# Mamba stages with compute engines kept in source order, lags of a slot or more between maker and reader, and one pair's X in SBUF

## The chip, the cores and the metric

The kernel runs on one core of a Trainium2 chip. The metric is the device time of one execution in microseconds (us). The core has five engines with a queue each: TensorE (PE, matmul), VectorE (DVE), ScalarE (ACT), GpSimd (POOL), and SyncE (SP), which here issues nearly all DMAs. An engine runs its queue in order; what it needs from another engine it waits for on a semaphore.

## The reference

Four layers over an image x of 4 x 96 x 64 x 64: a Mamba block with fusion and batch norm (layer 0), an SSD block (layer 1), a second Mamba block like the first (layer 2), a ConvNeXt block (layer 3). The change touches layers 0 and 2. With L = 4096 positions, DIN = 192, 16 states:

```python
def _mamba_block(seq, ...):
    h = (seq - mu) * rsqrt(var + EPS) * ln_g + ln_b
    xs, z = split(h @ in_w, 2)
    xc = silu(sum(conv_w[:, k] * xp[:, k:k + L, :] for k in range(4)) + conv_b)
    dbl = xc @ xproj_w                                  # dt (6), Bm (16), Cm (16)
    delta = softplus(dt @ dt_w + dt_b)
    dA = exp(delta[..., None] * A)
    dBx = delta[..., None] * Bm[:, :, None, :] * xc[..., None]
    hstates = associative_scan(dA, dBx)                 # h[t] = dA[t] * h[t-1] + dBx[t]
    y = (einsum('blds,bls->bld', hstates, Cm) + Dp * xc) * silu(z)
    return y @ out_w

for i in range(2):
    seq = seq + _mamba_block(seq, ...)
gp = relu(x.mean((2, 3)) @ gp_w.T + gp_b)               # one vector per image
out = fus_w @ concat([seq, gp]) + fus_b                 # then batch norm over all images
```

## The kernel before, in words

**Steps, groups, slots.** `mamba_fusion` (L467) keeps X, all four images as 96 channels x 4096, in SBUF. Images are handled in pairs. A step is one chunk of T = 512 positions of one pair in one of the two sub-layers: 2 pairs x 2 sub-layers x 8 chunks = 32 steps for each Mamba stage, 64 in the program. Two images of 192 channels fill three tiles of 128 partitions (j = 0, 1, 2). A step has 24 groups (`units`, L385), eight for each j; a group is two scans of 128 partitions (8 channels x 16 states) by 512. `Scan.run` (L383) writes the order of the work out by hand: it goes through slots n, one for each group, and in slot n calls the stages of different groups with fixed lags.

**The stages of a group g before** (lag in slots after its scan): `load` (-4) issues on SP the DMAs that broadcast 8 rows of delta (dd, written to DRAM by the front) over 16 states into da; a "DMA group" (6 of 24) also loads du from dg. `decay` (-2): ScalarE, two exps in place in da. `spread` (-1): for ordinary groups two matmuls (L313) that spread du into the PSUM tile bs; for DMA groups ScalarE's exps into bs and GpSimd's product du x B (L308). `scan` (0): for ordinary groups VectorE's product bs x B (L335), then two VectorE scans (L340) into hs, GpSimd's product hc = hs x C (L342), and ScalarE's copy of the last column into carry (L345). `sums` (+2): TensorE adds hc over states into py (L361); once per j a matmul adds D x xc (L355). `close` (+3): VectorE multiplies py by silu(z) (L369). `project` (+4): two matmuls into po (L377), VectorE adds po to X (L381). `fuse` (+5, second sub-layer only): matmul pf (L510), ScalarE adds the bias (L511), VectorE takes bn_stats (L512), SP stores.

**The front** (`mamba_front`, L155) makes the next step's tiles while this one scans. It is a generator; `PACE` (L256) says how many of its pieces each slot takes, and `LEAD` (L257) that it starts four slots before the step ends. Its pieces: layer norm (matmuls pc and pv, ScalarE's Square and rsqrt, VectorE's product L184, GpSimd's affine L185); twelve conv taps as matmuls (L194) with ScalarE copies into xz and a Silu; z (L204); the projection dbl (L217, L222), written to DRAM and read back broadcast as bc (L226, L245); and for each j softplus (L260): TensorE's pt, ScalarE's Abs, Exp, Ln, VectorE's max and add (L267), ScalarE's Identity back into the PSUM tile (L268), VectorE's second instruction (L270) on that PSUM tile and u, GpSimd's addition (L271) and product du (L248), and the stores dd and dg (L251).

**What sets the order.** The code is written against a framework that puts in semaphores and allocates buffers by name (`bufs` = how many; a new tile waits until the old one's users are done). It also sorts: each engine's queue is the result of a scheduler that may put a later instruction ahead of an earlier one that isn't ready by its own estimate. The lags and `PACE` are thus a wish; nothing before the change holds an engine to them.

## Time and profile before

| | |
|---|---|
| three runs | 9810.94, 9849.05, 9851.49 us (median 9849.05) |
| profiled execution | 9796.82 us, span 9795.1 us, mean granted TensorE clock 0.941 |
| busy, share of the span | PE 86%, DVE 83%, POOL 70%, ACT 56% |
| first Mamba stage | first scan at 78.1 us, batch norm's result at 3060 us |
| SSD stage | to about 6160 us |
| second Mamba stage | first scan at 6246 us, batch norm's result at 9210 us |
| ConvNeXt stage | to the end |
| DMA | 71% busy and 204 GB/s between 300 and 2700 us |

How to read the profile: a row of groups names line, engine, operation, output <- inputs, shapes and count; then busy us and mean ns of one; then the engine's idle time just before these instructions and what ended most of it. The slice rows cut the span into 40 equal parts; a digit is the busy share in tenths (9 is 90% or more). A row of a stretch (A:B) gives its length, then the busy us and number of instructions of PE, PE's weight loads, DVE, ACT and POOL, the granted clock, the DMA share and GB/s. A matmul of this kernel in fp32 is two records. A timeline row begins with start and length in us.

### The profile page before, as it was taken

How to read it: one execution, taken by the hardware profiler on the slowest of the kernel's cores; microseconds unless marked ns; L12 is line 12 of the kernel's file. 1: busy time of each engine (PE TensorE's matmuls, PEld its weight loads, DVE VectorE, ACT ScalarE, POOL GpSimd, SP SyncE). 2: the span in 40 equal slices, each digit the busy share in tenths (PEclk: the TensorE clock that was granted, in tenths of full speed). 3: DMA queues.
4: the chain of work that ended last, by engine and by line, in shares of the span. 5: the costliest groups of instructions: out<-in, count | busy, mean ns of one | idle time of the engine just before them, and what ended most of it. 6: DMA issues, size and time to landing. Idle time of an engine off the chain costs nothing. (4 is left out here: it accounts for less than half of the span.)

```text
span 9795.1 us, 110014 instructions
## 1 busy us (share of the span) xinstructions
PE 8426.9 (86%) x32750; PEld 3475.8 (35%) x32750; DVE 8142.4 (83%) x11036; ACT 5527.9 (56%) x10516; POOL 6879.1 (70%) x4573
## 2 busy tenths in 40 slices
PE   7888889888887988998888889788888888888678
PEld 1222212222212776776766767212212222222122
DVE  7999999999995666666666667699999999999887
ACT  5666666665663555555555555466666665666345
POOL 6888888888884555555555555588888888888511
PEclk8999999999997999999999999799999999999789
DMA  6677776777774222222222222576777776776653
GB/s 184 201 205 201 205 207 201 203 202 205 206 208 130 73 67 82 83 66 83 82 73 73 86 68 60 157 204 201 207 206 205 211 203 198 210 205 201 166 119 84
DMA packets 808930, 1525.65 MB, mean 156 GB/s; under 512 B 126190, under 2 KB 131722, under 8 KB 804491
## 3 DMA queue, kind: packets, MB, share of 16 engines
q1 hardware_dynamic: 805258, 1513.50, 54.4%
q8 instruction: 260, 4.26, 0.2%
q10 hardware_dynamic: 3072, 5.11, 0.1%
q14 instruction: 340, 2.78, 0.1%
HBM read 1222.99 MB, written 148.50 MB: 140 GB/s over the span
## 5 line engine op out<-in xcount | busy, mean ns | idle before, releaser
L342 POOL TENSOR_TENSOR hc<-hs,bc 128x1024 f32<-128x1024 f32 x1536 | 3610.9, 2358 | 625.5 <-DVE hs L340 545.8
L340 DVE TENSOR_TENSOR_SCAN hs<-da,carry,bs 128x512 f32<-128x512 f32 x2016 | 2466.5, 1264 | 81.0 <-DVE bs L335 2.8
L107 ACT ACTIVATE da<-da,w_a 128x512 f32<-128x512 f32 x2304 | 1616.9, 716 | 1251.7 <-DMA da<-dd 1191.7
L361 PE MATMUL py<-hc,selsum 128*32 128x512 f32 x6144 | 1797.8, 639 | 445.9 <-POOL hc L342 438.9
L313 PE MATMUL bs<-du,seldu 64*128 64x512 f32 x4608 | 1565.3, 675 | 216.0 <-DVE hs L340 203.7
L335 DVE TENSOR_TENSOR bs<-bs,bc 128x1024 f32<-128x1024 f32 x1152 | 1397.7, 1213 | 166.6 <-PE bs L313 163.1
L308 POOL TENSOR_TENSOR du<-du,bc 128x1024 f32<-128x1024 f32 x384 | 905.3, 2358 | 260.3 <-DMA du<-dg 141.0
L361 PEld LDWEIGHTS py<-hc,selsum 128*32 128x32 f32 x6144 | 239.8, 110 | 1791.8 <-POOL hc L342 1097.0
L917 DVE TENSOR_SCALAR seg<-dr,dac 128x128 f32<-128x128 f32 x1536 | 641.2, 451 | 281.9 <-PE y L962 279.5
L313 PEld LDWEIGHTS bs<-du,seldu 64*128 64x128 f32 x4608 | 444.0, 195 | 1205.2 <-DVE hs L340 864.4
L933 POOL TENSOR_TENSOR seg<-seg,cb 128x384 f32<-128x384 f32 x512 | 515.7, 1009 | 475.5 <-DVE cb L932 409.3
L194 PE MATMUL pu<-h,w_conv 96*128 96x512 f32 (+3 forms) x2048 | 833.4, 627 | 8.5 <-ACT rs L107 8.4
L340 DVE TENSOR_TENSOR_SCAN hs<-bs,carry,du 128x512 f32<-128x512 f32 x672 | 823.6, 1260 | 6.2 <-issue 3.2
L868 PE MATMUL front<-pk,sconv 128*128 128x512 f32 x1536 | 755.2, 609 | 27.7 <-ACT z L856 23.8
L972 POOL TENSOR_TENSOR y<-y,xs 128x192 f32<-128x192 f32 x496 | 295.3, 595 | 603.8 <-DVE y L971 587.9
L985 ACT ACTIVATE y<-yz 128x192 f32<-128x192 f32 x512 | 186.1, 363 | 906.2 <-DVE yz L984 905.5
L937 POOL TENSOR_TENSOR xs<-pre,coef 128x576 f32<-128x576 f32 x512 | 598.9, 1175 | 54.0 <-ACT pre L112 24.8
L879 PE MATMUL front<-sconv,pk 128*128 128x192 f32 x3072 | 572.0, 330 | 55.8 <-DVE pre L884 50.5
L345 ACT COPY carry<-hs 128x2 f32<-128x2 f32 x1344 | 250.9, 187 | 566.1 <-DVE hs L340 562.3
L879 PEld LDWEIGHTS front<-sconv,pk 128*128 128x128 f32 x3072 | 496.7, 190 | 87.7 <-DVE pre L884 76.8
L107 ACT ACTIVATE bs<-da,w_a 128x512 f32<-128x512 f32 x768 | 522.0, 680 | 3.1 <-DVE hs L340 1.6
L962 PEld LDWEIGHTS y<-xs,seg 128*128 128x128 f32 x3072 | 437.7, 204 | 142.0 <-issue 80.7
(209 smaller groups left out, 13623.5 us busy)
## 6 DMA issues: line engine op xcount, KB each, us to landing
da<-dd SPq DMA_DIRECT2D x3072, 256.0 KB
du<-dg SPq DMA_DIRECT2D x768, 256.0 KB
dr<-rows SPq DMA_DIRECT2D x256, 384.0 KB
bc<-rows SPq DMA_DIRECT2D x256, 256.0 KB
dd<-delta SPq DMA_DIRECT2D x192, 256.0 KB
dg<-du SPq DMA_DIRECT2D x192, 256.0 KB
pk<-xn SPq DMA_DIRECT2D x128, 384.0 KB
pk<-xn SPq DMA_DIRECT2D x128, 256.0 KB
```

Source lines behind the costliest of these rows:

```text
L107: self.last = self.scalar.activation(out, in_, func, **kw)
L194: nc.tensor.matmul(pu[r0:r1], lhsT=wt["conv"][:kk, tap, d0:d1], rhs=h[:kk, b, ds(tap, T)], start=(tap == 0), stop=(tap == 3),)
L308: nc.gpsimd.tensor_tensor(g["du"], g["du"], self.b_or_c(g, 0), ALU.mult)
L313: nc.tensor.matmul(g["bs"][:, i], lhsT=self.sel["du"][rows, g["half"], g["q"]], rhs=g["made"]["du"][rows, g["j"]], start=True, stop=True,)
L335: nc.vector.tensor_tensor(dbx, dbx, self.b_or_c(g, 0), ALU.mult)
L340: nc.vector.tensor_tensor_scan(hs[:, i], da[:, i], dbx[:, i], init, ALU.mult, ALU.add)
L342: nc.gpsimd.tensor_tensor(g["hc"], hs, self.b_or_c(g, 1), ALU.mult)
L361: nc.tensor.matmul(py[rows], lhsT=self.sel["sum"][:, g["q"]], rhs=g["hc"][:, i], start=(g["q"] == 0), stop=(g["q"] == NQU - 1),)
L868: nc.tensor.matmul(p, lhsT=self.conv[:, i, DI + q * DST : DI + (q + 1) * DST], rhs=pk[:, i, ds(c * T, T)], start=(i == 0), stop=(i == 2),)
L879: nc.tensor.matmul(p, lhsT=pk[:, i, ds(c * Q, Q)], rhs=self.conv[:, i, :DI], start=(i == 0), stop=(i == 2),)
L917: nc.vector.tensor_scalar(seg[:, h], g["pair"]["dr"][:, c % 2 * NH + h], made["dac"][:, n0 + h : n0 + h + 1], 0.0, ALU.subtract, ALU.min,)
L937: nc.gpsimd.tensor_tensor(xs, x.to_broadcast([P, 3, NH, HD]), coef.to_broadcast([P, 3, NH, HD]), ALU.mult)
```

## The change

Seven parts, all in the Mamba stages.

1. In `run`, after each slot, every instruction of the four compute engines is tied behind the one traced before it on its engine (`IN_ORDER`, an edge without a semaphore). SP isn't included.
2. Lags: load -5, hc and the carry copy become a stage of their own (`after`, +1), product du x B at -2, sums +3, close +4, project +4, `keep` +5, `spread_out` +6. Buffers: da 6 to 8, hs and hc 3 to 4, ua and lg 2. `LEAD` 5, other `PACE`.
3. The front's layer norm and softplus are skewed so that each piece reads what an earlier piece made. pv moves to the PSUM tile of po.
4. Softplus's Identity goes to an SBUF tile w instead of back into PSUM; VectorE's second instruction reads w and u.
5. The add into X is done by TensorE (identity x X into po first); ScalarE copies po to X. In the second sub-layer the fuse weight is multiplied into the out weight once, and fus x X takes the identity's place, so there is no fuse matmul.
6. bn_stats goes: sums come from ScalarE's accumulator outputs, squares from an added Square.
7. X holds one pair; pair 1's slices are loaded as pair 0's are finished, and the other pair's means come from pieces loaded through da tiles.

```diff
@@ mamba_front
-        sq = work.tile([P, T], F32, tag="ua", name="sq")[:C]
...
+    for n in range(4):
+        if n >= 2:
+            dst = h[:C, n - 2, 3 : 3 + T]
+            nc.vector.tensor_tensor(dst, centered[n - 2][0], roots[n - 2], ALU.mult)
...
+        if 1 <= n < 3:
+            pv = psum.tile([P, T], F32, tag="po", name="pv", bufs=1)[:C]
...
+        if n < 2:
+            pc = bank("pc")[:C]
...
     nc.scalar.activation(dbl, pd, AF.Identity, bias=wt["one"])
+    yield
...
+    for n in range(5):
+        if n >= 2:
+            j = n - 2
+            delta, lost = kept.pop(0)[:2]
+            nc.gpsimd.tensor_tensor(delta, delta, lost, ALU.add)
+            nc.gpsimd.tensor_tensor(du[:, j], delta, xz[:, j], ALU.mult)
...
+        if 1 <= n < 4:
+            softplus_rest(nc, *kept[-1])
...
+            kept.append(softplus(nc, k.act, work, pt))
@@
-PACE = (1,) * 8 + (2,) + (1,) * 7 + (2,) + (1,) * 7
-LEAD = 4
+PACE = (1,) * 5 + (2, 1, 1, 1) * 2 + (2,) + (1,) * 10
+LEAD = 5
@@ softplus
-    nc.vector.scalar_tensor_tensor(out, x, 0.0, t, ALU.max, ALU.add)
-    nc.scalar.activation(x, u, AF.Identity, bias=1.0)
-    nc.vector.scalar_tensor_tensor(t, x, 1.0, u, ALU.subtract, ALU.subtract, reverse1=True)
-    nc.gpsimd.tensor_tensor(out, out, t, ALU.add)
+    w = work.tile([P, T], F32, name="wa", bufs=2)
+    nc.scalar.activation(w, u, AF.Identity, bias=1.0)
+    return work.tile([P, T], F32, name="delta", bufs=2), t, u, w, x
+
+def softplus_rest(nc, out, t, u, w, x):
+    nc.vector.scalar_tensor_tensor(out, x, 0.0, t, ALU.max, ALU.add)
+    nc.vector.scalar_tensor_tensor(t, w, 1.0, u, ALU.subtract, ALU.subtract, reverse1=True)
@@ Scan
+    def product(self, g):
+        if g["dma"]:
+            self.tc.nc.gpsimd.tensor_tensor(g["du"], g["du"], self.b_or_c(g, 0), ALU.mult)
...
+    def after(self, g):
...
+        nc.gpsimd.tensor_tensor(g["hc"], hs, self.b_or_c(g, 1), ALU.mult)
...
@@ project
+        nc.tensor.matmul(po, lhsT=wt["of_x"], rhs=xs, start=True, stop=False)
...
-        nc.vector.tensor_tensor(xs, xs, po, ALU.add)
+    def keep(self, g, b):
+        xs = self.X[:, b, ds(g["c"] * T, T)]
+        if g["sub"] == 0:
+            self.tc.nc.scalar.copy(xs, self.po)
+        else:
+            self.fuse(g, b, xs, self.po)
@@ run
-                (self.load, -4), (self.spread, -1), (self.decay, -2), (self.scan, 0), (self.sums, 2),
+                (self.load, -5), (self.spread, -1), (self.decay, -2), (self.after, 1),
+                (self.product, -2), (self.scan, 0), (self.sums, 3),
...
+            for ins in traced[start:]:
+                if ins.engine not in self.engines:
+                    continue
+                if ins.engine in last:
+                    self.tc.add_manual_dep(ins, last[ins.engine].name, IN_ORDER, reason="order")
+                last[ins.engine] = ins
@@ mamba_fusion
-    X = one.tile([C, B, L], F32, name="X")
+    X = one.tile([C, 2, L], F32, name="X")
...
+    def fuse(g, b, xs, po):
+        nc.scalar.activation(
+            xs, po, AF.Identity, bias=gb[:, n // NT : n // NT + 1], accum_out=sums[:, n : n + 1]
+        )
+        nc.sync.dma_start(dst[n // NT, :, ds(g["c"] * T, T)], xs)
+
+    def spread_out(g, b):
+        nc.scalar.mul(means[:, n : n + 1], sums[:, n : n + 1], -1.0 / T)
...
+        nc.scalar.activation(
+            sq, xs, AF.Square, bias=means[:, n : n + 1], accum_out=squares[:, n : n + 1]
+        )
+        if g["pair"] == 0:
+            nc.sync.dma_start(xs, src[2 + b, :, ds(g["c"] * T, T)])
...
+    wts[0]["of_x"], wts[1]["of_x"] = k.ident[:C, :C], fus[:, 0]
+    for j in range(3):
+        nc.tensor.transpose(pt, wts[1]["out"][:, j], k.ident)
...
+        nc.tensor.matmul(pw, lhsT=turned, rhs=fus[:, 0], start=True, stop=True)
+        nc.scalar.copy(wts[1]["out"][:, j], pw)
```

## The prediction

> **What bounds the kernel now.** I read the page's busy rows first, then the busy time of two stretches in the middle of the two Mamba stages, then VectorE's (DVE's) groups and waits in the first of them, then a neighbouring stage for an operation that the change introduces.

> ```profile
> PE   7888889888887988998888889788888888888678
> DVE  7999999999995666666666667699999999999887
> POOL 6888888888884555555555555588888888888511
> ...
> 300.00:2700.00 2400.00, 2100.72 (x6432) 488.67 (x6432) 2245.83 (x2079) 1495.49 (x2675) 2055.48 (x987) 0.96 0.71 204
> ```

> The rows show two blocks where VectorE is at 9 tenths or more and TensorE (PE) and GpSimd (POOL) at 8; those are the Mamba stages, and the change touches nothing else. In the stretch 300 to 2700 us VectorE is busy 2245.8 of 2400 us. The same stretch holds 1247 scan instructions; a step (one chunk of 512 positions of one pair, 24 slots of two scans) has 48, so it is 25.98 steps, **92.4 us a step**, of which VectorE is busy 86.4. From 6400 to 9000 us, 1355 scans give 92.1. There are 64 steps: 64 x 92.2 = 5900 of the 9795 us span. VectorE's waits in the stretch:

> ```profile
> L335 DVE TENSOR_TENSOR bs<-bs,bc 128x1024 f32<-128x1024 f32 x467 | 566.7, 1214 | 70.5 <-PE bs L313 68.8
> L270 DVE SCALAR_TENSOR_TENSOR lg<-pt,ua 128x512 f32<-128x512 f32 x78 | 53.0, 680 | 16.6 <-ACT pt L268 16.1
> L381 DVE TENSOR_TENSOR X<-X,po 96x512 f32<-96x512 f32 x52 | 34.7, 668 | 10.9 <-PE bs L313 10.9
> L512 DVE BATCH_NORM_STATS2 stats<-X 96x6 f32<-96x512 f32 x24 | 16.1, 671 | 0.0
> ...
> DVE h L184 <- ACT rs L107: 12.1, 17, 1.4
> ...
> PE py L361 <- POOL hc L342: 165.9, 207, 4.6
> ```

> After the bar stand busy us and mean ns, then idle time before and its releaser. With the small ones VectorE's waits sum to 115 us, **4.4 a step**; 92.4 - 86.4 - 4.4 leaves 1.6 of gaps, mostly between the product at L335 and the scan that reads it. So VectorE sets the pace, with a twentieth lost, mostly to L313's matmul being late. The last line says why: that matmul queues on TensorE behind sums (L361) that wait for GpSimd's product hc, 165.9 us in this stretch.

> [...] in the SSD stage:

> ```profile
> L984 DVE TENSOR_TENSOR yz<-y,z x512: 336/1020/2630, 3158.0 to 6153.5; 128x192 f32<-128x192 f32 x171
> ...
> L971 DVE TENSOR_TENSOR y<-y,edac x496: 336/357/363, 3161.4 to 6152.1; 128x192 f32<-128x192 f32 x166
> ...
> 3253.30 1.15 POOL L937 TENSOR_TENSOR xs<-pre,coef 128x576 f32<-128x576 f32 x1
> 3253.64 1.02 DVE L984 TENSOR_TENSOR yz<-y,z 128x192 f32<-128x192 f32 x1
> 3254.41 0.62 POOL L981 TENSOR_TENSOR prev<-prev,dec 128x192 f32<-128x192 f32 x1
> ```

> Same shape, min/median/max ns: with both inputs in SBUF (L984) the median is 1020, with one in PSUM (L971) 357. The three rows below show one case: L984 begins under a GpSimd instruction that ends at 3254.45 and itself ends at 3254.66, 0.21 us later. The GpSimd instruction queued behind (L981, 0.50 alone) takes 0.62: VectorE went first. Of some 310 cases of a queued GpSimd instruction in this stage VectorE lost 7. In the Mamba stages no such VectorE instruction exists today (pt, po, pc, bs are PSUM), and every hc takes 2338 to 2388 ns. [...] L713 here has a median of 687 with both inputs in SBUF, so without contention the move from PSUM costs about 10 ns.

> **The change, part by part** (us per step).

> *Work taken off VectorE.* The add into X (L381) is two instructions of 0.668, bn_stats (L512) two of 0.671 in half of the steps, one on average. Neighbouring VectorE instructions start 0.08 before the end of the last, so each occupies 0.6: **-1.8**. Their replacements: one matmul more on TensorE (identity or fus times X: two added, the fuse matmul L510 dropped in half of the steps) at 0.97, the distance between matmul starts at 1500.5 to 1506.5 us; on ScalarE (ACT) per half-step a copy of about 0.58 (like L209), or for the last layer the same activation as today plus an accumulator read (0.19, like L985's), a mul (0.2) and a Square with accumulator (0.8), 1.8 on average. ScalarE is busy 57.5 of 92.4, TensorE 80.9: covered. Without cover the matmul would cost 1.0.

> *Softplus's second instruction* (L270, three a step) now reads w from SBUF instead of the copy in PSUM, so both inputs are in SBUF. In source order it comes 0.6 after the slot's last scan, and that scan's end has just released the 2.36 us product hc. First of the three: hc starts 0.17 after the scan, so 2.36 + 0.17 - 0.6 = 1.9 of waiting. Second and third: GpSimd is in the du multiplication (1.27) of the previous j, of which about 0.55 is left. Sum **+2.9**. Bounds: 0 if GpSimd is always idle there; 3 x 2.4 = 7.2 if each meets a fresh hc. [...] GpSimd loses about 0.5 each; it is busy 79.1 a step, so there is room.

> *Order and lags.* Sums go from two slots behind the scan to three, and hc is still released by the scan's end; with a slot of about 3.7 us (1.3 + 2.4) and hc at 2.4 to 4.7 (a du product in between in one slot of four) the 165.9 us of TensorE waiting loses its cause, and with it most of the 68.8 and 10.9. L270 no longer waits for the Identity of its own slot (16.1), and the layer norm product has a slot in hand (12.1). What is late next I work out from the queues: TensorE in slot order, against VectorE's 3.67 (ordinary slot), 2.36 (DMA slot), plus 0.6 per extra. In slots 0 and 8 TensorE has bs 1.06, sums 0.97, three project matmuls 2.9 and one of the front, 5.9 us against VectorE's 4.3; in slot 9 two conv taps follow. The matmul for the group after the next DMA slot then comes late: 0.7 in slot 10, 0.3 in slot 2, and some 0.3 for signals and a late exp: ScalarE's first copy into the new xz (slot 7) must wait until project of slot 8 has released that buffer, queued ahead of the exps of the next DMA group. New waits **1.3** (bounds 0.5, and today's 4.4): -4.4 + 1.3 = **-3.1**.

> *Product and scan are now always neighbours*: 18 pairs with at most 0.08 of gap, some of which are filled today: **+0.3**.

> *DMA.* Each step's 60 loads move from four to five slots ahead on SP's queue, with 8 buffers instead of 6; the load of group g takes a tile freed by scan g-7 or so, already done. Against the scans, rows and the four bc go one slot earlier and the six dd/dg stores stay where they were; on SP they wait for GpSimd, with loads queued behind: some 5 us, against 10 in hand before the exps. The store of X waits on ScalarE's new keep. Per stage 16 reloads of X (192 KB each, 3.1 MB) are added; the other pair's X, 3.1 MB, is no longer loaded up front but comes as eight pieces for its mean. 71% DMA busy leaves room: 0.

> *Once per stage*: three transposes, three matmuls and six copies ahead of the first scan, whose chain ends on SP issuing weights (to 74 us): +4 each, **+8** in all (bounds 0 and 20). The tail loses an add and a matmul (about 3.6 with hops) and gains the Square chain: 0.

> Sum: -1.8 + 2.9 - 3.1 + 0.3 = -1.7 a step, x 64 = -109, + 8 = **-101**. On the profiled execution's 9796.8 (its span and 1.7 around it) that is 9696; the median of the runs shown is 9849, 52 above, so I forecast 9849 - 101 = **9748**.

> **Rivals.**
> *A, the port costs little:* GpSimd is often idle at that moment, or the wait falls where VectorE would have waited for TensorE anyway: port 1.0, new waits 0.5. -1.8 + 1.0 - 3.9 + 0.3 = -4.4 a step, -282 + 8: **9575**. For it: GpSimd is idle 14% of the stretch. Against: in source order the scan that precedes softplus releases hc.
> *B, slower: in-order TensorE puts back the wait that the lag took away.* Place: slots 8 to 10 and 0 to 2, where six matmuls stand ahead of the next bs and no scheduler may pull bs forward. If waits stay at 4.4: -1.8 + 2.9 + 0 + 0.3 = +1.4, +90 + 8: **9947**. It decides from the point where new waits exceed 3.0 a step. For it: TensorE is busy 88% today. Against: the other 16 slots have at most 4.0 us of its work.
> *C, the order isn't imposed* on some engine, since it is only added edges and the scheduler sorts as now: edits -1.8, lag -1.5, port +2.0: -1.3, **9774**.

> **How the numbers follow.** Main case 0.50, A 0.22, B 0.20, C 0.08. A measurement of this kernel can tell about 0.5%, 49 us, from no change. Main, spread about 80 us around 9748: 0.39 faster, 0.10 same, 0.01 slower; A 0.22 faster; B 0.06 same, 0.14 slower; C 0.05 faster, 0.03 same. Together 0.66, 0.19, 0.15. The range runs from A's value to B's less a little, 9570 to 9930, leaving out about 0.1 on each side.

> **What would show it.** L381 and L512 gone from VectorE; about 90.5 us a step. The second softplus instruction well above 0.69 us on average (1.6 by my sum), its first of three near 2.6. TensorE's wait for hc near nothing, VectorE's for bs a third of today's, sitting after slots 0 and 8. Wrong if that instruction stays at 0.7 (A), or if VectorE's waits stay above 3.0 a step (B).

## The result and the profile after

The changed kernel takes **9990.72 us** (median of 4 runs, 9982.15 to 10006.38); the kernel before, 9845.95 (4 runs). The ratio is **1.0156**, interval 1.013 to 1.0183: slower by 1.6%, where 9748 was forecast. The profiled execution took 10006.38 us (span 10004.7), against 9796.82 before; the pair of profiles is thus 209.6 apart and the medians 145, since the profile of before lies 49 under its median and that of after 16 over. Sums from the traces below are held against the 209.6.

The slice rows of the changed kernel's page, in the order of those shown before, with the granted clock added:

```profile
PE   7888888888886988998988888788888888888678
DVE  7999999999996666666666667699899999899887
POOL 6888888888885555555555556588888888888611
PEclk8989999999997999999999999799989999899889
```

Some of VectorE's slices fell from 9 to 8, although its work per step should have become less. The stretch 300 to 2700 us again (length; then busy us and instructions of PE, PE's weight loads, DVE, ACT and POOL; clock, DMA share, GB/s):

```profile
300.00:2700.00 2400.00, 2064.35 (x6276) 473.66 (x6274) 2187.02 (x1935) 1430.24 (x2671) 2012.38 (x954) 0.91 0.75 198
```

It holds 796 + 265 + 108 + 36 = 1205 scans, 25.1 steps, so **95.6 us a step** against 92.4. VectorE is busy 2187.02 / 25.1 = 87.1 of them (86.4 before). Its groups other than the scans (busy us and mean ns, then idle time before and what ended it):

```profile
L366 DVE TENSOR_TENSOR bs<-bs,bc 128x1024 f32<-128x1024 f32 x452 | 548.4, 1213 | 25.5 <-PE bs L340 25.5
...
L296 DVE SCALAR_TENSOR_TENSOR lg<-wa,ua 128x512 f32<-128x512 f32 x75 | 86.9, 1158 | 8.5 <-DVE delta L294 0.5 <-ACT wa L288 0.5
L405 DVE TENSOR_TENSOR xz<-py,xz 128x512 f32<-128x512 f32 x75 | 51.7, 690 | 45.5 <-PE py L397 45.5
L294 DVE SCALAR_TENSOR_TENSOR delta<-pt,lg 128x512 f32<-128x512 f32 x75 | 50.5, 674 | 20.3 <-ACT lg L111 20.3
...
L178 DVE TENSOR_TENSOR h<-pc,rs 96x512 f32<-96x512 f32 x50 | 34.1, 682 | 56.4 <-ACT rs L111 56.3
```

The add and bn_stats are gone. Softplus's second instruction (L296) went from 680 to 1158 ns. The wait for bs fell from 68.8 to 25.5, but three others grew: the layer norm product for rs (12.1 to 56.3), close for py, softplus for lg. All of VectorE's waits together are 152 us, **6.05 a step** against 4.4. TensorE's wait for hc, 165.9 before, is gone: its sums now start with no idle time, and its waits are these (us, times, longest):

```profile
PE bs L340 <- DVE hs L371: 263.2, 101, 6.8
PE pv L184 <- ACT X L422: 39.3, 14, 2.8
PE pv L184 <- ACT X L564: 33.1, 11, 3.0
```

The last two are new and come once in each step. The timeline of the changed kernel shows one of them (start, length, what, idle time before it):

```profile
1507.72 1.10 PE L190 MATMUL pc<-X,center 96*96 96x512 f32 x2
...
1508.85 0.59 ACT L194 ACTIVATE sq<-pc 96x512 f32<-96x512 f32 x1 [6.29 <-PE pc L190]
1509.35 1.40 ACT L111 ACTIVATE bs<-da,w_a 128x512 f32<-128x512 f32 x2
1510.69 1.32 ACT L111 ACTIVATE da<-da,w_a 128x512 f32<-128x512 f32 x2
...
1511.91 0.18 ACT L381 COPY carry<-hs 128x2 f32<-128x2 f32 x1
1511.99 0.68 ACT L564 ACTIVATE X<-po,gb 96x512 f32<-96x512 f32 x1
...
1512.82 1.10 PE L184 MATMUL pv<-sq,mean 96*96 96x512 f32 x2 [3.02 <-ACT X L564]
...
1514.01 0.68 ACT L111 ACTIVATE rs<-pv,eps 96x512 f32<-96x512 f32 x1 [1.25 <-PE pv L184]
...
1514.79 2.08 PE L340 MATMUL bs<-du,seldu 64*128 64x512 f32 x4
...
1515.39 0.69 DVE L178 TENSOR_TENSOR h<-pc,rs 96x512 f32<-96x512 f32 x1 [2.01 <-ACT rs L111]
...
1516.92 1.23 DVE L366 TENSOR_TENSOR bs<-bs,bc 128x1024 f32<-128x1024 f32 x1 [0.84 <-PE bs L340]
```

pv now uses project's PSUM tile po. It cannot be written until keep (L564, or L422 in the first sub-layer) has copied po out, and keep is queued on ScalarE behind four exps and a carry copy: 3 us from sq's end. TensorE, held to its order, waits 3.02; the bs matmuls behind pv wait with it and then take 2.08 us, against 1.13 elsewhere (see the last section). VectorE then waits 2.01 for rs and 0.84 for bs. My theory was therefore: **the shared bank behind keep** costs most; second is what the prediction calls the port, L296 with both inputs in SBUF at 1158 ns against L270's 680 with one. The rivals: the imposed order as such; ScalarE's largest wait, the copy into xz (269.0 us in the stretch, up to 12.6 at once); and a TensorE slowed by its granted clock, which fell from 0.96 to 0.91.

### The profile page after: what moved, and what is told of

Its sections match the earlier page's. It is cut to its first block, busy times and chain, and to the rows that moved or that the text cites. A ratio compares the mean times of both kernels' runs of the same rounds, so it can differ in the third digit from the quotient of the medians.

```text
span 10004.7 us, 110143 instructions
## 1 busy us (share of the span) xinstructions
PE 8518.0 (85%) x32896; PEld 3506.5 (35%) x32896; DVE 8183.2 (82%) x10870; ACT 5507.8 (55%) x10786; POOL 6946.7 (69%) x4573
## 5 line engine op out<-in xcount | busy, mean ns | idle before, releaser
L378 POOL TENSOR_TENSOR hc<-hs,bc 128x1024 f32<-128x1024 f32 x1536 | 3662.6, 2390 | 672.3 <-DVE hs L371 663.5
L340 PE MATMUL bs<-du,seldu 64*128 64x512 f32 x4608 | 1517.4, 712 | 719.8 <-DVE hs L371 719.7
L397 PE MATMUL py<-hc,selsum 128*32 128x512 f32 x6144 | 1736.7, 649 | 9.2 <-POOL hc L378 9.2
L111 ACT ACTIVATE da<-da,w_a 128x512 f32<-128x512 f32 x2304 | 1521.1, 710 | 1.5
L340 PEld LDWEIGHTS bs<-du,seldu 64*128 64x128 f32 x4608 | 406.0, 202 | 1703.3 <-DVE hs L371 1128.5
L348 POOL TENSOR_TENSOR du<-du,bc 128x1024 f32<-128x1024 f32 x384 | 932.7, 2429 | 0.0
L974 PE MATMUL front<-sconv,pk 128*128 128x192 f32 x3072 | 572.8, 330 | 55.5 <-DVE pre L979 50.2
L1057 PEld LDWEIGHTS y<-xs,seg 128*128 128x128 f32 x3072 | 439.3, 205 | 140.7 <-issue 79.1
L210 ACT COPY xz<-pu 128x512 f32<-128x512 f32 x192 | 111.3, 580 | 653.1 <-PE po L415 637.2
```

The costliest lines, as they stand in the source:

```text
L111: self.last = self.scalar.activation(out, in_, func, **kw)
L340: nc.tensor.matmul(g["bs"][:, i], lhsT=self.sel["du"][rows, g["half"], g["q"]], rhs=g["made"]["du"][rows, g["j"]], start=True, stop=True,)
L348: self.tc.nc.gpsimd.tensor_tensor(g["du"], g["du"], self.b_or_c(g, 0), ALU.mult)
L378: nc.gpsimd.tensor_tensor(g["hc"], hs, self.b_or_c(g, 1), ALU.mult)
L397: nc.tensor.matmul(py[rows], lhsT=self.sel["sum"][:, g["q"]], rhs=g["hc"][:, i], start=(g["q"] == 0), stop=(g["q"] == NQU - 1),)
L974: nc.tensor.matmul(p, lhsT=pk[:, i, ds(c * Q, Q)], rhs=self.conv[:, i, :DI], start=(i == 0), stop=(i == 2),)
```

## The experiments

Each ratio is against the kernel before, on the same chip. The runs e1 to e4, e5 to e8, e9 to e12 and e13 to e16 were on four chips, so runs of different groups are compared by their ratios and not by their times. Short names are used in the text. In the expectations, which were written before each run, ORDER means that fixed queues make engines wait, PORT that softplus's second instruction, with both inputs in SBUF, is held up by GpSimd's instructions (1158 ns against 680), and CLOCK that TensorE is slower because its granted clock fell (0.96 to 0.91).

| run | edit | median us | ratio (95%) |
|---|---|---|---|
| e1 | after, no order edges | 9911.06 | 1.0088 (1.006 to 1.0115) |
| e2 | after, second softplus instruction reads PSUM | 9941.98 | 1.0127 (1.0104 to 1.015) |
| e3 | after, three xz buffers | 10001.05 | 1.0188 (1.0165 to 1.0212) |
| e4 | after, keep ahead of the slot's exps | 9862.27 | 1.0042 (1.0026 to 1.0058) |
| e5 | before, order edges alone | 10927.04 | 1.1127 (1.1106 to 1.1148) |
| e6 | e4, sums ahead of bs on TensorE | 9967.83 | 1.0158 (1.0139 to 1.0176) |
| e7 | e6, w in PSUM | 9825.67 | 1.0008 (0.9999 to 1.0016) |
| e8 | after, ScalarE's order free | 10203.0 | 1.0399 (1.0377 to 1.0421) |
| e9 | e4, w in PSUM | 9792.4 | 0.9969 (0.996 to 0.9978) |
| e10 | e9, no order edges | 9749.08 | 0.992 (0.9902 to 0.9938) |
| e11 | e9, close between product and scans | 9741.58 | **0.9919** (0.9903 to 0.9934) |
| e12 | e9, VectorE's add back, no identity matmul | 9780.1 | 0.9957 (0.9943 to 0.9971) |
| e13 | e9, VectorE's add back, matmul kept | 9818.31 | 0.9998 (0.9989 to 1.0007) |
| e14 | e11 and e12 together | 9760.1 | 0.9943 (0.9929 to 0.9957) |
| e15 | e11, no order edges | 9747.26 | 0.9927 (0.9915 to 0.994) |
| e16 | e9 on the chip of e13 to e15 | 9785.53 | 0.9968 (0.9956 to 0.9981) |

**Is it the order, the port, the xz buffer, or keep?**

e1, the edges left out:

```diff
-            for ins in traced[start:]:
+            for ins in ():
```

> The changed kernel without its order edges: lags, pieces, buffers and VectorE work as changed, but the scheduler sorts the four queues again. Theory ORDER (the fixed queues make ScalarE and TensorE wait for each other in the slots of the layer norm, of project and of softplus, and VectorE pays 6.0 us a step for it): about 9750, faster than the 9846 of before. Rival CLOCK (TensorE is slower because its granted clock fell from 0.96 to 0.91): clock and time stay, about 9950 to 9990. Rival PORT [...]: at least 9900, since the port conflict stays.

Faster than the change by 0.7%, but slower than before and far from ORDER's 9750; PORT's bound of 9900 held. VectorE's wait for rs and TensorE's for keep are gone, 82.0 us of waiting for bs are back, and L296 rose to 1504 ns. So the order costs something here, and the changed layout is slower than before without it too.

e2, one of the two SBUF inputs taken out of softplus's second instruction:

```diff
-    nc.vector.scalar_tensor_tensor(t, w, 1.0, u, ALU.subtract, ALU.subtract, reverse1=True)
+    nc.vector.scalar_tensor_tensor(t, x, 1.0, u, ALU.subtract, ALU.subtract, reverse1=True)
```

> The changed kernel, but softplus's second VectorE instruction reads the PSUM tile pt where it read w, so it has one SBUF input (this leaves the rounding correction of softplus out: a wrong small term is added instead). PORT: the instruction falls from 1158 to about 690 ns, 1.4 us a step, and GpSimd is no longer delayed: 90 us or more, to 9900 or below. ORDER: the 1.4 us a step mostly turn into other waits, 9930 to 9990.

The instruction, in the groups of e2, takes 692 ns, near the 680 of the kernel before:

```profile
L296 DVE SCALAR_TENSOR_TENSOR lg<-pt,ua 128x512 f32<-128x512 f32 x77 | 53.3, 692 | 2.6
```

Of the 1.4 us a step, 90 us in 64 steps, that this frees, about a third shows in the medians (1.0156 to 1.0127), and the intervals overlap, so that even this is not certain. The waits for rs and bs grew from 81.8 to 111.3 us in the stretch, while that for py fell from 45.5 to 28.9. With other waits behind it, the price of L296 is at least partly hidden.

e3, a third xz buffer, to take away ScalarE's longest wait:

```diff
-    xz = made["xz"] = work.tile([P, 6, T], F32, name="xz", bufs=2)
+    xz = made["xz"] = work.tile([P, 6, T], F32, name="xz", bufs=3)
```

> The changed kernel with three xz buffers instead of two, so that ScalarE's first copy into xz needn't wait for project of the step before last (10.7 us of ScalarE waiting a step). ORDER in its form 'ScalarE held by xz': 60 to 120 us faster. Rival: that wait lies in ScalarE's slack and VectorE's waits stand elsewhere: within 20 us of 9991.

ScalarE's wait for project's po is gone and nothing is gained: it was slack, and VectorE's waits stay (rs 58.1, py 40.1, bs 33.3, lg 20.4).

e4, keep called ahead of the stages of its slot, so that ScalarE has it before that slot's exps; nothing else moves:

```diff
+            if (g := at(5)) and g["last"] and g["j"]:
+                self.keep(g, g["j"] - 1)
...
-            for lag, what in ((4, self.project), (5, self.keep), (6, self.spread_out)):
+            for lag, what in ((4, self.project), (6, self.spread_out)):
```

> The changed kernel, but keep is put first in its slot on ScalarE, ahead of the exps, so that TensorE's pv needn't wait for it (2.9 us of TensorE waiting a step, behind which rs and the layer norm product come late by 2.2). ORDER: 1.5 to 2 us a step, about 9880. CLOCK: no change, 9991 within 20.

From 1.0156 to 1.0042, some 112 us, about what ORDER said and against CLOCK's "no change". VectorE's waits in e4:

```profile
DVE xz L405 <- PE py L397: 38.7, 67, 2.0
DVE hs L371 <- issue: 24.4, 43, 1.0
DVE delta L294 <- ACT lg L111: 15.8, 19, 1.1
DVE hs L371 <- POOL hc L378: 6.1, 9, 0.8
...
DVE h L178 <- ACT rs L111: 0.6, 3, 0.2
```

rs fell from 56.3 to 0.6 and bs is no longer among them. The place of keep on ScalarE, twice in each step, carries the largest part of the loss; that cause is shown. VectorE's waits still sum to 88 us, 3.4 a step.

**The order by itself.** e5 puts the edges of part 1 on the kernel before, whose lags stay as they were:

```diff
+            for ins in traced[start:]:
+                if ins.engine not in self.engines:
+                    continue
+                if ins.engine in last:
+                    self.tc.add_manual_dep(ins, last[ins.engine].name, IN_ORDER, reason="order")
+                last[ins.engine] = ins
```

> The kernel before with the order edges alone, nothing else changed. ORDER: here stages read what their own slot makes, so a fixed order must cost more than it did after the change was laid out for it: 2 to 5% slower, above 10000. Rival: the scheduler's order is about the source's order anyway, within 0.5% of before.

11% slower, more than twice the most that was expected. Pieces that read what their own slot makes now stall VectorE, as its two longest waits in e5 show:

```profile
DVE delta L270 <- ACT lg L110: 185.8, 60, 5.5
DVE bs L340 <- PE bs L318: 65.6, 19, 3.6
```

These waits point to parts 2 and 3 as what makes part 1 bearable; but e5 lacks parts 4 to 7 too, and no run separates them. e8 leaves ScalarE alone out of the order (the other three engines were not tried):

```diff
-        self.engines = [e.engine for e in (nc.tensor, nc.vector, nc.scalar, nc.gpsimd)]
+        self.engines = [e.engine for e in (nc.tensor, nc.vector, nc.gpsimd)]
```

> The changed kernel with TensorE, VectorE and GpSimd held in order and ScalarE sorted by the scheduler. ORDER in its form 'ScalarE's fixed order is at fault': the layer norm product's wait for rs (2.2 us a step) and softplus's wait for Ln go, at most 9900 on the scale where the changed kernel has 9991. If TensorE's order is at fault instead: within 30 us of the changed kernel.

Slower than the change by 2.4%, a miss: the wait for lg rose from 20.3 to 66.7, and those for rs (57.0) and py (55.7) stayed or grew. A likely reason, which no run tests, is that the scheduler places ScalarE's work by its own estimate of the other engines, which are no longer where it puts them.

**What is left after keep: close, and the second SBUF input.** e6 puts the sums ahead of bs on TensorE, so that py is ready for close:

```diff
-                (self.load, -5), (self.spread, -1), (self.decay, -2), (self.after, 1),
-                (self.product, -2), (self.scan, 0), (self.sums, 3),
+                (self.load, -5), (self.sums, 3), (self.spread, -1), (self.decay, -2), (self.after, 1),
+                (self.product, -2), (self.scan, 0),
```

> keep first on ScalarE, and on TensorE the sums ahead of the spread matmuls, so that TensorE fills the time in which it waits for a scan and py is ready for close. ORDER: close's wait (38.7 us of 2400 with keep first, 1.5 us a step) goes: 80 to 110 us below keep first alone, a ratio to before of 0.994 to 0.997. CLOCK: close is late because TensorE is slow after idling; the wait stays, ratio 1.002 to 1.005.

A miss: close's wait is gone, and the loss is back. TensorE now waits for close (py behind xz, 106.8 us) with bs queued behind it, and VectorE waits for bs (28.4) and for GpSimd's hc (68.2). L296 rose to 1492 ns.

e7 adds to e6 that w is written to PSUM, to project's tile:

```diff
-    w = work.tile([P, T], F32, name="wa", bufs=2)
+    w = psum.tile([P, T], F32, tag="po", name="wa", bufs=1)
```

> The kernel e6, and w is written into the PSUM bank of po, free in softplus's slots, so that the second VectorE instruction has one SBUF input. PORT: that instruction falls from 1208 to about 690 ns, 1.5 us a step: 60 to 100 us below e6, ratio to before about 0.987. Rival (the port wait only changes places, or the single bank makes ScalarE wait for VectorE): no gain on e6.

1.5% under e6, with L296 down from 1492 to 692 ns. That is more than the 60 to 100 us expected, which started from 1208 ns; the expected ratio of 0.987 is missed by 1.4%, since it was built on the gain that e6 did not bring. e9 is the same edit on e4:

> The two repairs together, without the moved sums: keep ahead of the exps (as in e4_keep_first), and softplus's w in the PSUM bank that project uses (as in e7). Theory, the shared bank and the port are separate costs that both lie on VectorE's path: softplus's second instruction falls from 1208 ns to about 692, 1.5 us a step or some 100 us, so from 9862 of e4 to about 9760, a ratio to the kernel before of 0.993 (0.988 to 0.998). Rival, the time goes to another wait as it mostly did in e2: within 0.2% of e4, 1.002 to 1.006, with VectorE's waits for the sums or for bs larger by what the instruction gives up.

Faster than the kernel before, 0.7% under e4 and inside the range that the theory gave: 72 us for 64 x 3 x (1208 - 692) ns = 99 us of instruction time, so that most of the price of L296 now shows. The group in e9:

```profile
L296 DVE SCALAR_TENSOR_TENSOR lg<-wa,ua 128x512 f32<-128x512 f32 x78 | 54.0, 692 | 8.8 <-ACT da L111 0.5 <-DVE delta L294 0.5
```

e11 moves close behind the product of its slot instead of moving the sums:

```diff
             nc.vector.tensor_tensor(dbx, dbx, self.b_or_c(g, 0), ALU.mult)
+        if self.due:
+            self.close(self.due)
```

> The kernel of e9 with close put between the product and the scans of its slot, so that the py it reads has 1.2 us more to arrive. Theory, the 1.5 us a step that VectorE waits for py is lost time: that wait falls below 0.4 a step and the kernel is 0.5 to 0.8% faster than e9. Rival, TensorE cannot go on with the next sums until close has read py, so the wait moves to TensorE and from there to the next bs: within 0.2% of e9, with VectorE's waits for bs larger.

0.5% under e9, with the lowest ratio here. The wait for py, 55.5 us in e9, is gone; but 22.1 of waiting for bs come in, the scans' wait for hc grows from 8.9 to 42.1, and their wait without a releaser in the profile (issue) from 25.3 to 48.5. VectorE's waits together are 107 us in e9, 4.1 a step, and 116 in e11, 4.4 a step. The gain that the theory forecast came, but not as less waiting: the gaps fell from 2.4 to 2.0 us a step and the busy time from 85.5 to 85.0. Why is open. e10 and e15 are e9 and e11 with the edit of e1:

> The kernel of e9 with the order edges left out, so that the scheduler orders the engines again. Theory, the imposed order itself costs nothing once no instruction waits in it for what its own slot makes: the free order is slower than e9 by 0.5 to 1.5%, with VectorE waiting for bs again (2 to 3.5 us a step). Rival, the imposed order is what costs, as the step from the changed kernel to e1 suggests (0.7%): the free order is faster than e9 by 0.5% or more.

> e11 without the order edges. Theory, in e10 the scheduler gained 0.5% over e9 only because it could move close and the sums apart, which e11 does by hand: e15 within 0.2% of e11 or slower. Rival, the imposed order costs something more (gaps, or TensorE's waits for the scan): 0.4% or more faster than e11, 0.988 or less.

e10 is 0.5% under e9, against my theory: with keep moved and w in PSUM the scheduler does better than the written order, as long as close waits in it. e15 and e11 cannot be told apart (intervals overlap), as e15's theory said, and e10 lies with them; the free order ends at the same time with other waits (bs 54.0, py 35.3, rs 23.3 in e15). The profiles show where the two orders differ. From its first to its last scan a Mamba stage takes 2913 and 2914 us in e11 and 2929 and 2927 in e15. But the first scan of all starts at 90.8 us in e11 and at 78.4 in e15, and the second stage too starts some 13 us later behind the SSD stage. So the written order loses at the start of a stage what it wins in the steps. This is one profile of each; e9 and e16, which are one kernel, differ by up to 10 us in a stage.

**What the work taken off VectorE was worth.** e12 puts the add of the first sub-layer back on VectorE and drops the identity matmul; e13 keeps the matmul, against a matrix of zeros:

```diff
-            self.tc.nc.scalar.copy(xs, self.po)
+            self.tc.nc.vector.tensor_tensor(xs, xs, self.po, ALU.add)
```

> The kernel of e9 with the residual of the first layer added by VectorE again, as in the kernel before (two adds of 0.6 us in half of the steps, 64 adds in all), and TensorE's identity matmul left out. It prices the work that the change took off VectorE. Theory, VectorE is on the path: 64 x 0.6 = 38 us slower than e9, a ratio higher by 0.3 to 0.5%. Rival, TensorE is as close to the path as VectorE: its matmul less (64 x about 1 us) gives back what the add costs, within 0.15% of e9.

> The kernel of e12 with TensorE's third matmul of project kept, against a matrix of zeros, so that against e9 only VectorE's 64 adds of 0.6 us come on top (and ScalarE's copies go). Theory, VectorE's own work is on the path and in e12 the matmul that went paid for it: 38 us slower than e9, a ratio higher by 0.3 to 0.5%. Rival, VectorE waits that much less elsewhere (in e12 its waits fell by 0.4 us a step): within 0.15% of e9, and the waits for py, lg and the scans' buffers are shorter by what the adds take.

> The kernel of e9 on the chip of e13 to e15, so that these are compared on one chip. Expected 0.9969 again, within 0.15%.

e12 is no slower than e9 (0.9957 against 0.9969; the intervals overlap): in the first sub-layer the exchange of VectorE's add for TensorE's matmul gained nothing that these runs can tell. e13 is slower than e9 on its chip (e16) by 0.30%, 30 us for 64 adds: 0.46 us each, for the add and its wait together. And e13 is 0.41% slower than e12, 40 us for 64 matmuls: 0.63 us each. But in e13 VectorE's add waits for that matmul, 34.3 us in the stretch against 9.8 in e12:

```profile
DVE xz L405 <- PE py L397: 47.2, 57, 3.4
DVE X L422 <- PE po L415: 34.3, 28, 1.8
```

In the changed kernel a copy on ScalarE stands in the add's place. The 0.63 us is therefore the matmul's price in e13's layout, and what it costs in the changed kernel was not measured apart.

> e11 and e12 together: close between product and scans, and the first layer's residual added by VectorE again, without the identity matmul. If the two act apart, e11's ratio 0.992 less what e12 gained over e9 (0.1%): 0.990 to 0.992. Rival, once close's wait is gone VectorE has no slack left and the adds show in full: 0.995 to 0.997.

0.9943, between both theories' numbers and 0.2% over e11, with overlapping intervals: whether the exchange of add for matmul pays beside e11 stays open.

## Why the prediction was wrong

Its own terms, us a step of the first stage, from the two traces:

| term | predicted | measured |
|---|---|---|
| work taken off VectorE | -1.8 | -2.0: (34.7 + 16.1) / 25.98 |
| second softplus instruction | +2.9 | +1.4: 3 x (1158 - 680) ns |
| waits | -3.1 (to 1.3) | +1.65 (to 6.05) |
| gaps | +0.3 | +0.85 (1.6 to 2.45) |
| less overlap of neighbours, scans | 0 | +1.3: the rest of VectorE's busy time, 86.4 to 87.1 |
| sum | -1.7 | +3.2 |

The 1.8 of the forecast had overlap with neighbours taken off already and the 2.0 has not; the difference is in the row on overlap. That row can be checked by sums: VectorE's groups add up to 2328.8 us for 2245.8 of busy time before, and to 2238.1 for 2187.0 after, so overlap fell from 3.2 to 2.0 us a step.

64 x 3.2 = 205 is near the 209.6 between the profiled executions, but that is in part chance. From the first scan with a carry to the last scan the two stages are longer by 83 and 97 us, 180 together; the last two steps of a stage became shorter, by 8 and 7 us. Starting the stages costs 7 and 8, by the first scan with a carry (185.4 instead of 178.3 us in the first), where 4 each was forecast. The SSD stage, whose code is the same, is 17 longer in this pair of profiles; over all profiles here it takes 3004 to 3042 us, and 3030 and 3005 in e9 and e16, which are one kernel. So these 17 lie within what the same code varies by.

**The step that failed** is the waits, "New waits **1.3** (bounds 0.5, and today's 4.4)". It rests on "the layer norm product has a slot in hand (12.1)". A slot in hand is worth nothing if the maker is held up: the prediction follows pv to its reader and not to its buffer. The diff moves pv into po's bank; po is released by keep; keep is queued on ScalarE behind the exps. I listed what ScalarE gained as "covered" by its busy share and did not ask when keep runs. A lag of a slot between maker and reader covers data, and this wait is for a buffer. e4 shows it: keep moved and nothing else, 112 us, and the waits for rs and bs (2.2 and 1.0 a step) gone. With close (1.8) and lg (0.8) they are nearly all of the 6.05. The measured 6.05 lies beyond the upper bound, which took today's waits as the worst case for a layout with other queues.

**Rival B** had nearly the size (9947, decided from 3.0 of waits) and the mechanism in part, an in-order TensorE that may not pull bs forward. Its place was wrong: the wait begins with pv and not with the six matmuls of slots 0 and 8, and bs itself waits 1.0 a step. Its second part is close (1.8 a step): TensorE's sums arrive late for it, which I did not queue. Moving close (e11) gained 0.5%, though not as less waiting in all.

**The port**, as the prediction calls it, was right in kind, half in size: 1.4, not 2.9. No trace shows a port, only how long instructions take. e9 shows that it is the second SBUF input: with w in PSUM the same instruction takes 690 to 693 ns, against a median of 971 and a longest of 2900 in the changed kernel. That GpSimd is the other party shows in e1's trace, in the same stretch: the 24 of these instructions that began while GpSimd ran nothing took 691 ns on average, and the other 54 ended 0.55 us after the GpSimd instruction under which they began. In the changed kernel all 75 began under one and ended 0.55 us after it, by the median. L984 in the SSD stage of before agrees: the 85 that began while GpSimd ran nothing took 342 to 360 ns, the other 427 a median of 1020. The size was off because less of it was left: the first of three took 1.47 us on average and not 2.6, as its hc had 0.93 us to go and not 1.9, and the others met 0.40 of a du product and not 0.55.

**Work off VectorE** was right as busy time, but its worth is not borne out: e9, with the exchange in the first sub-layer, is no faster than e12 without it. So "TensorE 80.9: covered" was more than a busy share can say. How the loss splits between the matmul and the rest is not shown for the changed kernel, and bn_stats and the second sub-layer were not tried.

**Right, and not enough for the result:** TensorE's wait for hc is gone, and VectorE's for bs fell to about the third that was forecast (25.5 of 68.8); ScalarE's copy into xz does wait for project (10.95 us at 1541.50), and e3 shows that nothing hangs on it.

With keep moved, w in PSUM and close moved, the change reaches 0.9919. That this is close to the 0.9897 of the forecast is luck: the forecast charged 2.9 us a step for softplus's second instruction, which e11 does not pay (692 ns). The gaps and the lost overlap are not explained by any run here.

## What to carry to other kernels

Before a lag is counted as slack, follow each tile to its buffer's last user as well as to its maker, and write down what is queued ahead of that user on its engine. When queues are held in order, give a short-lived tile no bank that a copy behind long work releases, and test each moved instruction alone: one place in one queue was worth 1.1% here. A busy share does not show that added work is covered on an engine that others wait for; put the work back and measure the exchange.

## What the runs showed of the hardware

```profile
1579.67 1.13 PE L340 MATMUL bs<-du,seldu 64*128 64x512 f32 x4
...
1590.29 2.08 PE L340 MATMUL bs<-du,seldu 64*128 64x512 f32 x4 [6.47 <-DVE hs L371]
```

The wait there is 6.47 us; shorter waits are followed by half speed too. In the timeline above TensorE waits 3.02 us, the granted clock is 1.00 from 1511.2 to 1514.5 us and 0.50 from 1514.6 to 1517.9, and bs takes 2.08. In the stretch all 25 groups of bs that began after more than 6 us of idling took 2.08 us, all 23 after 2 to 3 us took 1.53 or more, and of the 326 after none to speak of (up to 0.1 us) 14 took over 1.5. The granted clock in the stretch fell from 0.96 to 0.91. Behind the wait of 6.47 us the four matmuls thus took 0.95 us longer; how much of the loss such delays are, no run isolates. A lower clock alone does not make the kernel slower than before: e11 is faster at 0.94, against 0.96.

GpSimd's instructions were longer too: hc took 2391 ns on average and the product of du 2431 with w in SBUF, 2355 both in e9. By the means, that is (603 x 36 + 151 x 76) ns / 25.1 = 1.3 us a step, near the 0.5 for each of three that the prediction gave, and about as much as VectorE's own 1.4.
